# A graph-attention and expert kernel: 14 instead of 15 gathers per source block, and a new order in TensorE's step

## The chip, the cores and the metric

The program runs on one core of a Trainium2 chip. The metric is the time of one execution on the device in microseconds, as the median of several runs. A profile is one execution, taken with the hardware profiler, and has a time of its own.

## The reference

A graph of 6250 nodes with 256 features and 100,000 edges goes through a two-head graph attention layer and then through a layer of eight experts, each with a layer norm ahead and a residual.

```python
x = x + gat(layernorm(x), edge_index)      # W: 256 -> 2 heads of 128
x = x + ffn(layernorm(x))                  # 256 -> 1024, gelu, 8 experts

# gat
Wh = (x @ W_w + W_b).reshape(N, H, D)
s, t = Wh @ a[:D], Wh @ a[D:]
e = leaky_relu(s[src] + t[dst], 0.2)
alpha = softmax of e over the edges of each src
agg = segment_sum(alpha * Wh[dst], src)    # nodes without edges keep Wh

# ffn
H = gelu(x @ W1 + b1)
probs = softmax(H @ Wg + bg)
out = probs[best] * (H @ Wd[best] + bd[best])   # the best expert only
```

The edges come sorted by dst, and dst is skewed to low numbers: about a fifth of the edges go to the first 256 nodes.

## The kernel before

**Preparation.** The edges are spread over the 128 partitions, and each partition sorts its own by source block (128 source nodes) and dst. Meanwhile every node's projected row, with its attention factors, goes to a table in HBM (260 floats a row).

**The edge loop.** The 49 source blocks are worked one after the other. For each, an indirect DMA fetches the 44 keys of every partition that belong to the block (`window`, L615). Up to four edges per partition that go to hot nodes (dst below 256) are handled as counts, without a gather (`pick_pairs`, `count_pairs`, `weigh_pairs`, `add_pairs`). The others are gathered from the table, one indirect DMA for 128 edges, one per partition: a column. There are T = ND + NC columns. The first ND = 12 hold a partition's first 12 edges "in place". What a partition has beyond these is "late": late edges of all partitions are counted (`prefix`), ranked, and packed into NC = 3 more columns of 128 slots. `split` (L657) makes a 0/1 matrix `pick` of late slots by partition, `gather_late` (L733) multiplies it with the keys on TensorE, one product for each late column, and `choose` (L740) takes the one key out of every row and writes its dst and its place.

`spread` (L758) transposes the places on TensorE, stores them in HBM and loads them back broadcast to all partitions (`lbc`). `compare` (L769) makes a 0/1 matrix of it, and `factors` (L773) multiplies this with the source terms; `factor_sums` (L782) adds up their three parts. `fetch` (L788) issues the gathers in three thirds, split at QS, into one of five `wg` buffers of five columns. `compare_back` and `weigh` scale the gathered rows, and `add_up` (L828) sums them by source node, two records on TensorE for each column.

**The expert work.** Four blocks make a group k. When its last block is finished (slot v), the group is normed, transposed (`g_turn`), multiplied with W1 (`g_hidden`), its expert is chosen, and its rows are transposed (`g_rows`) and sent to lists by expert (`g_send`). `tabulate` (L1065) finds which list tiles are full. Such tiles are loaded (`w_load`), transposed (`w_turn`), multiplied with their expert's weights (`w_expert`) and turned into output rows (`w_out`, L1151), which for all but the last two groups go to a waiting place and are sent at the end.

**The order.** No scheduler orders this. Every piece is entered with `at(slot, place, fn, ...)`, the list is sorted by slot and then place, and each engine and each DMA queue works its instructions in that order. A block takes three slots: u = 3 b. Within a slot the places run from about 5 to 81. So for block b: `gather_late` in slot u - 3, `choose` and `spread` in u - 2, `compare`, `factors` and `count_pairs` in u, `factor_sums` in u + 1, and thirds of `fetch` in u, u + 1 and u + 2, of `weigh` one slot and of `add_up` three slots later. At the end `judge` (L719) checks that no block has more late edges than slots (NS = NC x 128); if one has, the program runs a general path after the common one.

Of the kernel before, what the change touches and what calls it, by code (L numbers as in the profile page):

```python
# [10 lines left out]
F32 = mybir.dt.float32  # L11
# [12 lines left out]
P = 128  # L24
# [12 lines left out]
def common_path(  # L37
# [30 lines left out]
    NX = Wg.shape[1]  # L68
# [10 lines left out]
    assert KR * KQ == ES  # L79
    HB, HK = 2, 4  # L80
    HOT = HB * P
    ND, NC, WIN = 12, 3, HK + 40
    NR = WIN - HK - ND
    KS = ES + WIN
    NS = NC * P
# [9 lines left out]
    NPH = -(-(NB - 1) // FB) + 1  # L95
# [6 lines left out]
    NMAX = 2 * NX  # L102
# [91 lines left out]
    with ExitStack() as edges:  # L194
# [3 lines left out]
        def at(slot, place, fn, *args):  # L198
            plan.append((slot, place, len(plan), fn, args))

        kp = edges.enter_context(tc.tile_pool(name="keyp", bufs=2))
# [3 lines left out]
        fw = edges.enter_context(tc.tile_pool(name="ffnw", bufs=2))  # L205
# [118 lines left out]
        bufs = [None] + [keyb if i % 2 == 0 else keya[:, :ES] for i in range(len(steps))]  # L324
# [186 lines left out]
        for i, (d, flip) in enumerate(steps):  # L511
            t = 11 + 1.7 * i if i < 18 else 41.6 + 1.02 * (i - 18)
# [16 lines left out]
        for f0, f1, t0, step in ((n0, n1, 8.0, 0.7), (n4, NB - 1, 15, 2.0)):  # L529
            for j, b in enumerate(range(f0, f1)):  # L530
                c = b % CH
                t = t0 + step * (j - 0.5 * c)
# [11 lines left out]
        for b in range(NB):  # L544
            t = XN0 + NODE * b
# [194 lines left out]
        def choose(b):  # L740
            k = kept[b]
            loc, dsti = k["loc"], k["dsti"]
            pk = k["pm"][:, :NC * (NR + 1)].rearrange("p (c r) -> p c r", c=NC)
            col = kp.tile([P, NC], F32, name="col")
            nc.vector.tensor_sub(col, slot_of, pk[:, :, NR])
            hit = kp.tile([P, NC, NR], F32, name="hit")
            nc.vector.tensor_tensor(hit, iota_s[:, :NR].unsqueeze(1).to_broadcast([P, NC, NR]),
                                    col.unsqueeze(2).to_broadcast([P, NC, NR]), op=ALU.is_equal)
            nc.vector.tensor_mul(hit, hit, pk[:, :, :NR])
            got = kp.tile([P, NC], F32, name="got")  # L750
            nc.vector.tensor_reduce(got, hit, AX.X, ALU.add)
            got_i = got.bitcast(I32)
            nc.vector.tensor_scalar(dsti[:, ND:], got_i, 8, 0x1FFF, op0=ALU.logical_shift_right, op1=ALU.bitwise_and)
            late_i = kp.tile([P, NC], I32, name="late_i")
            nc.vector.tensor_single_scalar(late_i, got_i, 255, op=ALU.bitwise_and)
            nc.scalar.copy(loc[:, ND:], late_i)
# [308 lines left out]
        def tabulate(k, n, last):  # L1065
# [14 lines left out]
            shift = fw.tile([P, NX], F32, name="shift")  # L1080
            nc.vector.tensor_sub(shift, done, upto[:, :NX])
            nc.vector.tensor_add(done, shift, upto[:, 1:])
            past = fw.tile([P, NMAX, NX + 1], F32, name="past")[:, :n]
            nc.vector.tensor_tensor(past, upto.unsqueeze(1).to_broadcast([P, n, NX + 1]),
                                    iota_s[:, :n].unsqueeze(2).to_broadcast([P, n, NX + 1]), op=ALU.is_le)
            tab_f = fw.tile([P, 2, NMAX], F32, name="tab_f")[:, :, :n]
            nc.vector.tensor_reduce(tab_f[:, 0, :], past[:, :, 1:], AX.X, ALU.add)
            which = fw.tile([P, NMAX, NX], F32, name="which")[:, :n]
            nc.vector.tensor_sub(which, past[:, :, :NX], past[:, :, 1:])
            pickd = fw.tile([P, NMAX, NX], F32, name="pickd")[:, :n]  # L1090
            nc.vector.tensor_mul(pickd, which, shift.unsqueeze(1).to_broadcast([P, n, NX]))
            nc.vector.tensor_reduce(tab_f[:, 1, :], pickd, AX.X, ALU.add)
            nc.vector.tensor_add(tab_f[:, 1, :], tab_f[:, 1, :], iota_s[:, :n])
# [96 lines left out]
        for b in range(NB):  # L1190
            u = 3 * b
            at(u - 6, 46, window, b)
            at(u - 4, 24, measure, b)
            at(u - 4, 43, prefix, b)
            at(u - 3, 5, prefix_out, b)
            at(u - 3, 12, split, b)
            at(u - 3, 33.7, gather_late, b)
            at(u - 2, 17, pick_pairs, b)
            at(max(u - 1, -0.2), 63, load_terms, b)
            at(u, 56, scale_terms, b, 0)  # L1200
            at(u + 1, 56, scale_terms, b, 1)
            at(u, 34, count_pairs, b)
            at(u + 2, 51, weigh_pairs, b)
            at(u + 4, 31, add_pairs, b)
            at(u - 2, 16, choose, b)
            at(u - 2, 33.5, spread, b)
            at(u, 9, compare, b)
            at(u, 33, factors, b)
            at(u + 1, 47, factor_sums, b)
            at(u + 4, 62, owned, b)  # L1210
            at(u + 6, 13, owned_biased, b)
            for q in range(3):
                at(u + q, 30, fetch, b, q)
                at(u + q + 1, 48, compare_back, b, q)
                at(u + q + 1, 50, weigh, b, q)
                at(u + q + 3, 32, add_up, b, q)
            at(u + 6, 14, finish, b)

        worked = n_off = 0
        u = [3 * blocks_of(k)[-1] + 6 for k in range(NPH)]  # L1220
        for k in range(NPH):
# [35 lines left out]
            for i in range(n):  # L1257
                t = v + 15 + i if last else u[k + 1] + (5 + 8 * i // n if k < NPH - 2 else (10, 11, 12, 13, 14)[i])
                at(t - 1 if last else t - 2 if k == NPH - 2 else max(t - 3, v + 15), 46 if last else 64, w_load, k, i)
                at(t, 21, w_turn, k, i)  # L1260
                at(t + 1, 22, w_expert, k, i)
                at(t + 2, 30 if k < NPH - 2 else 36, w_out, k, i)
                at(t + 2, 45, w_send if k >= NPH - 2 else w_wait, k, i)
        at(v + 18, 47, judge)
        for j in range(-(-n_off // 2)):
# [539 lines left out]
```

## Time and profile before

| what | us |
|---|---|
| median of three runs | 1344.82 |
| lowest and highest | 1343.49, 1346.52 |
| the profiled execution | 1348.73 |
| its span, first to last instruction | 1346.9 |
| gathers (L792): first and last start | 114.7, 1193.1 |

The span falls into three parts: the preparation up to the first gather, the edge loop with the expert work of earlier groups beside it, and a tail after the last gather, which holds the last group. Between starts of a block's window gather (L619) at 265.9 and 1067.8 lie 36 blocks in 801.9 us, 22.3 us a block. Granted clock of TensorE: 0.924 on the mean, 0.82 between 265.9 and 353.6 us, 0.98 between 708.6 and 796.3 us.

In the profile a gather's row on GpSimd (POOL) is the time in which GpSimd makes the DMA; the transfer itself is not in it. "Issue" as a reason for idle time means that the engine waited for nothing that the profile shows. A matmul in float32 shows as two records on TensorE, each with a weight load (PEld).

### The profile page before, as it was taken

What the parts mean: (1) busy time and instruction counts of PE and PEld (TensorE: products, weight loads), DVE (VectorE), ACT (ScalarE), POOL (GpSimd) and SP (SyncE); (2) the same over time, 40 slices, a digit from 0 to 9 for tenths busy, and PEclk for the clock granted to TensorE, in tenths of its full rate; (3) what the DMA queues carried; (4) which work ended last, traced back from release to release, by engine and by line L of the source; (5) the groups of instructions that cost most, each with busy time, mean ns of one, the idle gap of its engine ahead of it and who ended that gap; (6) DMA issues with size and microseconds to landing.
All of it is one profiled execution on the core that took longest, in us unless ns stands there. A gap on an engine that the chain in (4) does not pass through costs nothing. (4 is left out here: it accounts for less than half of the span.)

```text
span 1346.9 us, 22461 instructions
## 1 busy us (share of the span) xinstructions
PE 1130.7 (84%) x6404; PEld 864.5 (64%) x6404; DVE 945.8 (70%) x3521; ACT 694.2 (52%) x2060; POOL 877.9 (65%) x990
## 2 busy tenths in 40 slices
PE   4683667777986998989979989899898998998997
PEld 3462555556674775775856757757676677585785
DVE  6986877868687787786777876968777779652311
ACT  4683344544645455546465565564645555645321
POOL 0005777777777777776777777777776767736362
PEclk9796887897997998998999999999998899899998
DMA  4764776765656566665766656666657566646871
GB/s 143 220 198 133 228 208 168 207 195 152 187 156 204 182 204 181 221 180 178 219 208 186 216 172 199 198 203 202 213 178 208 158 193 190 182 155 236 296 251 54
DMA packets 118428, 257.91 MB, mean 191 GB/s; under 512 B 24254, under 2 KB 70538, under 8 KB 118152
## 3 DMA queue, kind: packets, MB, share of 16 engines
q0 software_dynamic: 46544, 137.57, 34.2%
q1 hardware_dynamic: 64440, 111.76, 26.3%
q10 hardware_dynamic: 7312, 7.05, 1.6%
q8 instruction: 55, 0.90, 0.3%
q14 instruction: 77, 0.63, 0.2%
HBM read 205.03 MB, written 57.98 MB: 195 GB/s over the span
## 5 line engine op out<-in xcount | busy, mean ns | idle before, releaser
L792 POOL DMA_INDIRECT wg<-table,dsti x735 | 717.0, 976 | 238.4 <-issue 190.4
L833 PE MATMUL p_a<-wg,hot 128*128 128x258 f32 x1470 | 365.5, 399 | 0.0
L833 PEld LDWEIGHTS p_a<-wg,hot 128*128 128x128 f32 x1470 | 286.5, 201 | 52.0 <-issue 9.2
L826 ACT ACTIVATE wg<-wg 128x128 f32<-128x128 f32 x735 | 230.9, 390 | 4.8
L916 PE MATMUL pf<-xT,w_sb 128*128 128x512 f32 (+1 forms) x416 | 200.1, 630 | 22.7 <-ACT xT L908 22.7
L1146 PE MATMUL pf<-wd_sb,half 128*128 x880 | 206.3, 388 | 0.0
L1146 PEld LDWEIGHTS pf<-wd_sb,half 128*128 128x128 f32 x880 | 163.9, 191 | 37.0 <-issue 11.6
L824 ACT COPY wg<-fix 128x10 f32<-128x10 f32 x147 | 25.0, 170 | 297.0 <-DVE wg L823 232.2
L916 PEld LDWEIGHTS pf<-xT,w_sb 128*128 128x128 f32 x416 | 81.3, 210 | 109.5 <-issue 80.6
L809 DVE TENSOR_TENSOR hot<-fix,loc 128x640 f32<-128x640 f32 x147 | 119.1, 810 | 32.7 <-ACT wg L824 32.7
L823 DVE TENSOR_TENSOR wg<-wg,fix 128x640 f32<-128x640 f32 x147 | 120.7, 821 | 5.1
L918 ACT ACTIVATE hT<-pf,b_sb 128x512 f32<-128x512 f32 (+1 forms) x104 | 67.9, 659 | 55.1 <-PE pf L916 54.9
L1040 ACT COPY half<-pf 128x512 f32<-128x512 f32 x110 | 61.4, 585 | 65.9 <-PE pf L1146 34.3
L1040 ACT COPY row<-pf 128x512 f32<-128x512 f32 x94 | 52.4, 586 | 55.0 <-PE pf L1039 54.5
L1060 POOL DMA_INDIRECT by_expert<-row,place_i x47 | 46.8, 996 | 51.1 <-ACT half L1040 17.5
L771 DVE TENSOR_SCALAR lbc<-lbc,iota_p 128x1920 bf16<-128x1920 bf16 x49 | 36.1, 737 | 61.2 <-DMA lbc<-lrow 61.2
L456 PE MATMUL pf<-w_sb,xT 128*128 128x260 f32 x196 | 61.1, 441 | 19.0 <-ACT xT L450 19.0
L704 ACT ACTIVATE wt<-tm,hot_e 128x128 f32<-128x128 f32 x196 | 66.5, 386 | 8.1 <-DMA tm<-terms 8.1
L1039 PE MATMUL pf<-ident,hT 128*128 128x128 f32 x392 | 59.3, 289 | 13.3 <-ACT row L1040 13.2
L619 POOL DMA_INDIRECT win<-keys,first x49 | 48.5, 989 | 32.1 <-DMA keys<-keyb 14.2
L1039 PEld LDWEIGHTS pf<-ident,hT 128*128 128x128 f32 x392 | 46.8, 148 | 21.3 <-ACT row L1040 18.5
L1039 PE MATMUL pf<-ident,row 128*128 128x128 f32 x312 | 45.2, 283 | 18.1 <-DVE y L1160 12.4
(274 smaller groups left out, 1746.9 us busy)
## 6 DMA issues: line engine op xcount, KB each, us to landing
row<-by_expert SPq DMA_DIRECT2D x39, 641.0 KB
lbc<-lrow SPq DMA_DIRECT2D x49, 480.0 KB
wg<-table,dsti POOLq DMA_INDIRECT x735
wg<-by_expert SPq DMA_DIRECT2D x16, 641.0 KB
wd_sb<-in_L_ffn_Wd_dram SPq DMA_DIRECT2D x8, 1024.0 KB
tm<-terms SPq DMA_DIRECT2D x49, 128.0 KB
table<-tb ACTq DMA_DIRECT2D x12, 520.0 KB
xs<-in_x_dram SPq DMA_DIRECT2D x12, 512.0 KB
```

The source lines that it names most:

```text
L456: nc.tensor.matmul(pW[:, :TW], xT[:, k * P:(k + 1) * P], w_sb[:, k, :], start=(k == 0), stop=(k == KC - 1))
L704: nc.scalar.activation(kept[b]["wt"][:, g, h, :], tm[:, h, :], AF.Identity, scale=hot_e[:, g, 1, h:h + 1])
L792: nc.gpsimd.indirect_dma_start(out=wg[:, t - QS[q], :], out_offset=None, in_=table[:, :], in_offset=bass.IndirectOffsetOnAxis(ap=kept[b][" ...
L809: nc.vector.tensor_tensor(hot[:, :n], iota_ps.unsqueeze(1).to_broadcast([P, n, P]), kept[b]["loc"][:, QS[q]:QS[q + 1]].unsqueeze(2).to_bro ...
L823: nc.vector.tensor_mul(wg[:, :, :D], wg[:, :, :D], p_w[:, :, 0:1].to_broadcast([P, n, D]))
L826: nc.scalar.activation(wg[:, t, D2:SE], wg[:, t, D2:SE], AF.Identity, scale=wg[:, t, D + 1:D2])
L833: nc.tensor.matmul(sums[b], hot[:, t - QS[q], :], wg[:, t - QS[q], :SE], start=(t == 0), stop=(t == T - 1))
L916: nc.tensor.matmul(ph[:, :w], wt["w1"][:, k, j * P:(j + 1) * P], xT[:, k, :w], start=(k == 0), stop=(k == KC - 1))
L918: nc.scalar.activation(hT[:, j, :w], ph[:, :w], AF.Gelu, bias=wt["b1"][:, j:j + 1])
L1039: nc.tensor.transpose(pT[:, j * P:(j + 1) * P], rows(4 * h + j), ident)
L1040: nc.scalar.copy(o, pT)
L1146: nc.tensor.matmul(py[:, :C], res[k]["half", i, j // 4][:, j % 4, :], wt["wd"][:, ds(wo[0] + j * C, C)], start=False, stop=(j == KH - 1))
```

## The change

ND goes from 12 to 8 and NC from 3 to 6: T from 15 to 14 columns, NS from 384 to 768 late slots, NR, the keys of a partition that can be late, from 28 to 32. The thirds of `fetch` stay 5, 5 and, now, 4 columns, so columns 8 and 9, the first two late ones, come in the second third. Four work tiles have one buffer instead of two. Six entries of the order move within their slot: `gather_late` from place 33.7 to 40, `spread` from 33.5 to 40, `factors` from 33 to 42, `count_pairs` from 34 to 43, `factor_sums` from 47 to 10, and `w_out`, for all groups but the last two, from 30 to 11.

```diff
-    ND, NC, WIN = 12, 3, HK + 40
+    ND, NC, WIN = 8, 6, HK + 40
     NR = WIN - HK - ND
     KS = ES + WIN
     NS = NC * P
...
-            hit = kp.tile([P, NC, NR], F32, name="hit")
+            hit = kp.tile([P, NC, NR], F32, name="hit", bufs=1)
...
-            past = fw.tile([P, NMAX, NX + 1], F32, name="past")[:, :n]
+            past = fw.tile([P, NMAX, NX + 1], F32, name="past", bufs=1)[:, :n]
...
-            which = fw.tile([P, NMAX, NX], F32, name="which")[:, :n]
+            which = fw.tile([P, NMAX, NX], F32, name="which", bufs=1)[:, :n]
...
-            pickd = fw.tile([P, NMAX, NX], F32, name="pickd")[:, :n]
+            pickd = fw.tile([P, NMAX, NX], F32, name="pickd", bufs=1)[:, :n]
...
-            at(u - 3, 33.7, gather_late, b)
+            at(u - 3, 40, gather_late, b)
...
-            at(u, 34, count_pairs, b)
+            at(u, 43, count_pairs, b)
...
-            at(u - 2, 33.5, spread, b)
+            at(u - 2, 40, spread, b)
             at(u, 9, compare, b)
-            at(u, 33, factors, b)
-            at(u + 1, 47, factor_sums, b)
+            at(u, 42, factors, b)
+            at(u + 1, 10, factor_sums, b)
...
-                at(t + 2, 30 if k < NPH - 2 else 36, w_out, k, i)
+                at(t + 2, 11 if k < NPH - 2 else 36, w_out, k, i)
```

## The prediction

> **What bounds the kernel now.** I read the page's first lines, then the costliest groups, then windows cut where a block begins, then the waits of GpSimd and TensorE inside those windows, and last TensorE's timeline over one block. The page comes first only to see that no engine looks full.
>
> ```profile
> span 1346.9 us, 22461 instructions
> ...
> PE 1130.7 (84%) x6404; PEld 864.5 (64%) x6404; DVE 945.8 (70%) x3521; ACT 694.2 (52%) x2060; POOL 877.9 (65%) x990
> ```
>
> GpSimd at 65% is misleading. Its gathers are the group with the largest busy time, and the idle time ahead of them is nearly all "issue", that is, no other engine is named:
>
> ```profile
> L792 POOL DMA_INDIRECT wg<-table,dsti x735 | 717.0, 976 | 238.4 <-issue 190.4
> L833 PE MATMUL p_a<-wg,hot 128*128 128x258 f32 x1470 | 365.5, 399 | 0.0
> ```
>
> In the timeline one gather starts each 1.25 us: 0.95 us busy and 0.30 us of issue. So a stretch with 70 GpSimd instructions is full at about 87.5 us. I cut windows at every fourth window gather (L619), since the feed-forward work returns every four blocks. The columns are length, then busy time and count of each engine, then clock and DMA:
>
> ```profile
> 353.60:440.80 87.20, 71.65 (x408) 53.17 (x407) 66.86 (x253) 46.58 (x140) 66.90 (x70) 0.88 0.58 175
> 708.60:796.30 87.70, 78.69 (x478) 60.35 (x477) 68.14 (x257) 48.67 (x142) 66.31 (x71) 0.98 0.65 201
> 796.30:886.00 89.70, 80.60 (x488) 61.41 (x487) 69.00 (x258) 50.34 (x150) 65.89 (x70) 0.98 0.63 197
> ```
>
> The first is GpSimd's pace and nothing else; TensorE has 15.6 us to spare. In the other two TensorE is busy 79 to 81 us of 88 to 90. Over the long middle stretch (266 to 1068 us) the waits of GpSimd and of TensorE are:
>
> ```profile
> POOL wg L792 <- issue: 138.1, 448, 0.8
> POOL wg L792 <- ACT wg L824: 9.6, 14, 1.8
> POOL by_expert L1060 <- ACT row L1055: 4.6, 3, 2.4
> ```
>
> ```profile
> PE pm L761 <- ACT loc L756: 23.8, 11, 5.7
> PE pf L916 <- ACT xT L908: 17.6, 9, 2.0
> PE pf L1039 <- DVE y L1160: 11.1, 7, 2.3
> PE pm L779 <- DVE lbc L771: 9.0, 3, 4.5
> ```
>
> GpSimd hardly waits, so it sets the pace. TensorE waits little and is second, close behind. The timeline shows what its steps cost and where it waits for the late places (L761):
>
> ```profile
> 862.96 2.34 PE L833 MATMUL p_a<-wg,hot 128*128 128x258 f32 x10
> 865.13 0.52 PE L779 MATMUL pm<-src_term,lbc 128*128 128x6 bf16 x15
> 865.51 0.83 PE L738 MATMUL pm<-rest,pick 128*128 128x29 f32 x6
> 866.18 0.61 PE L691 MATMUL pm<-places,dests 128*128 128x128 bf16 x8
> ...
> 871.80 0.28 PE L761 MATMUL pm<-ident,loc 128*15 128x128 f32 x1 [1.89 <-ACT loc L756]
> ```
>
> **What the Trainium skill says.** "DMA: Bandwidth & Descriptors", section "SWDGE vs HWDGE vs iDMA", says that GpSimd builds the descriptors of its DMAs in software, and indirect DMAs are its own. The trace agrees: 0.95 us of GpSimd per gather whatever else runs. "TensorE: Matmul & The Clock Gate", section "LDWEIGHTS", says that a weight load costs by its columns. The trace agrees: the six late-rank records (29 moving columns, 128 weight columns) start 0.67 us ahead of the next group, 0.11 us each, as the 128-column transposes of L1039 do in the tail (8 in 0.87 us). So a late column is paid by its weights. "Perfetto Trace Analysis", section "Identifying the Most-Contended Engine", warns that TensorE's busy share is no good measure of its room; I therefore work with its waits.
>
> **The change, part by part.**
>
> GpSimd: 49 gathers less (735 to 686), 1.25 us each: 61 us of its queue, 5.0 us per four blocks.
>
> TensorE, per block: the gather's two records go, at 0.217 us each (ten from 862.96 to 865.13), -0.43 us; one of 15 factor matmuls goes, 0.38 us / 15, -0.03 us. Three late-rank products of two records each are added at 0.11 us, +0.67 us; 33 columns instead of 29 cost nothing while the weights set the pace. Sum +0.21 us a block, +0.84 us per four.
>
> VectorE, per block, by slopes between rows of the by-form groups (384 elements 422 ns and 28 elements 181 ns for a TENSOR_SCALAR; 128 elements 347 ns and 384 elements 621 ns for a SCALAR_TENSOR_TENSOR; 84 elements 248 ns and 640 elements 810 ns for a TENSOR_TENSOR): the two picks over 768 columns +0.26 and +0.41 us; three operations over 192 elements instead of 84, +0.11 us each; the last third's two wide operations over 512 instead of 640 elements, -0.13 us each; compare -0.05 us. Sum +0.7 us. ScalarE loses one 0.39 us scaling. VectorE is busy 68 us of 88, so I charge nothing; the cover is its own waits (48 us for lbc and 43 us for the late counts in the middle stretch). Without the cover it would be 2.8 us per four blocks.
>
> One buffer instead of two (hit, past, which, pickd): all their readers and writers are VectorE, in order. Nothing.
>
> spread from 33.5 to 40: it issues a transpose, a ScalarE copy and two DMAs on SP. Between the two places nothing is issued on SP or GpSimd (GpSimd's fetch is at 30, its send at 44, SP's store at 45), so it passes only g_fold, g_count, g_turn and g_rows on TensorE and their copies on ScalarE. In the slot after a group is finished, VectorE runs the norm and the table ahead of choose, and TensorE stood 1.8 us for loc with transposes ready behind it; these now go first. The price is a later lbc: spread to compare takes about 8 us where compare waits (899.3 to 907.4), and spread moves some 2.5 us later in two of four blocks. Compare would then wait 1 to 2 us more there, ahead of split; the late-count wait that follows takes most of it.
>
> gather_late, factors and count_pairs to 40 to 43: none of them issues a DMA, and in their slot nothing of TensorE lies between the old and new places except in the last group. Late ranks now precede factors, so choose's input comes no later than 0.3 us. Nothing.
>
> factor_sums from 47 to 10: it waits for factors, the end of TensorE's slot before. Queued behind are w_out, choose and pick_pairs, and spread waits for choose. But choose waited for the same end already. I take 0; bounds 0 and +0.6 us a block (the count_pairs group, if it waits for that too).
>
> w_out from 30 to 11: its PSUM buffer comes free before choose or split runs, not after. TensorE's waits for "DVE y" are 2.1 us of the period at 708 to 796 us (1.6 at L1039, 0.5 at L903). I let both go; bounds 0 and -2.1 us.
>
> The late columns are now in the second third's gathers (columns 8 and 9), a slot sooner. The late places (L756) were ready 10 us or more before that fetch in every block but the first, where it was 5. Nothing.
>
> **The sum.** Between 705 and 800 us the groups of TensorE show 9.1 us of waits: 2.0 for xT, 1.4 for row copies, 2.5 at the row transposes, 1.8 for loc, 0.5 and 0.7 at L903 and L1144, 0.2 at L650. The change takes 1.8 + 2.1 = 3.9 us, so TensorE needs 87.7 - 3.9 + 0.84 = 84.6 us. GpSimd would need 87.5 - 5.0 = 82.5 us. TensorE ends last there: -3.1 us per dense period. Blocks 2 to 8 (seven) and 9 to 16 (eight) have TensorE to spare: 15 x 1.25 = 18.8 us. Blocks 0 and 1, part of it: 1 us. Blocks 17 to 48 are eight dense periods: 8 x 3.1 = 24.8 us. Head (to 115 us) and tail (from 1194 us, a chain of expert products) are as before. Sum 44.6 us. The profiled execution took 1348.7 us (span 1346.9 and 1.8 around it), 3.9 above the median of the runs. 1348.7 - 44.6 = 1304.1; against the median 1344.8 - 44.6 = 1300.
>
> **Rivals.** (A) The forecast, TensorE takes over: 1300, own range 1288 to 1312. Chance 0.50.
>
> (B) GpSimd stays the bound since TensorE's busy time is partly drain: 61.5 us plus about half of the 14 us in which GpSimd now waits for others, 1276; with all of it 1269. For it: L779's 0.52 us group leaves room for the next after 0.38. Against: four waits of TensorE stay. 0.20.
>
> (C) The moves free nothing and TensorE keeps its 9 us of waits: -19.8 + 8 x 0.84 = -13, so 1332. For it: xT and the row copies are not touched, and VectorE now stands at the head of each slot. 0.18.
>
> (D) Slower: the late places sit last in TensorE's slot, lbc lands later, compare is first in VectorE's slot and holds split, and the products last in TensorE's slot then wait for split and compare. This decides once TensorE's waits per dense period grow from 9.1 by over 1.6 us (19.8 / 8 - 0.84). At 1 us a block, +4: 8 x 4.84 - 19.8 = +19, so 1364. For it: compare waited 17 times, up to 4.5 us. Against: after it VectorE waits for the late counts anyway. 0.10.
>
> (E) A block's late edges overflow its 768 slots and the general path runs: from the inputs the fullest block has 760. 0.02, far slower.
>
> **Numbers.** About 0.2% (2.7 us) is what can be told from no change. A, B and nearly all of C are faster: 0.86; same 0.03; slower 0.11. The range, 1270 to 1328, holds A, B and half of C.
>
> **What would show it.** 686 gathers still 1.25 us apart early; a window of four blocks near 82.5 us at 350 us and 84 to 85 us after 600 us; the loc wait of TensorE under 5 us in the middle stretch, the DVE y wait gone, xT as before; GpSimd waiting for ScalarE and TensorE more than now. If the dense windows read 82.5, B; if 88 with TensorE's waits kept, C; if lbc and L738 waits grow, D.

## The result and the profile after

| | before | after |
|---|---|---|
| median of 22 runs | 1346.25 us | 1352.35 us |
| lowest and highest | 1337.12, 1354.38 | 1338.90, 1358.21 |
| ratio after to before, 95% interval | | 1.0041 (1.0019 to 1.0063) |
| the profiled execution, its span | 1348.73, 1346.9 | 1348.91, 1347.1 |

The changed kernel is slower by 0.4%, where 1300 us was forecast. The two profiled executions lie nearer together than the medians do (0.2 us against 6.1), so the traces below show where the expected 44.6 us went, not all of the 6 us.

The page of the changed kernel, first lines and the two groups that were shown of before:

```profile
span 1347.1 us, 22591 instructions
...
PE 1141.0 (85%) x6551; PEld 878.2 (65%) x6551; DVE 974.3 (72%) x3521; ACT 675.3 (50%) x2011; POOL 840.9 (62%) x941
...
L792 POOL DMA_INDIRECT wg<-table,dsti x686 | 675.0, 984 | 260.8 <-issue 192.4
L833 PE MATMUL p_a<-wg,hot 128*128 128x258 f32 x1372 | 345.5, 401 | 0.0
```

The work moved as written: GpSimd (POOL) 37 us less, TensorE (PE) 10 us and VectorE (DVE) 28.5 us more. Windows of four blocks, cut at the window gathers as before (length first, then each engine's busy time and count):

```profile
341.70:425.20 83.50, 69.74 (x385) 53.06 (x385) 67.65 (x244) 44.33 (x134) 64.13 (x67) 0.90 0.58 175
696.80:787.90 91.10, 82.14 (x501) 63.05 (x500) 70.05 (x256) 49.26 (x147) 62.58 (x67) 0.98 0.60 183
787.90:880.20 92.30, 83.03 (x496) 63.85 (x496) 70.93 (x258) 48.32 (x144) 62.98 (x66) 0.94 0.60 184
```

The first is GpSimd's new pace, 67 instructions of 1.25 us, down from 87.2. The dense windows were 87.7 and 89.7 and became 91.1 and 92.3. A block is taken to start at its window gather. Block by block: block 17 starts 15.6 us earlier than before (425.2 against 440.8), block 45 only 7.6 us earlier (1060.2 against 1067.8), block 48 4.1 us, the last scatter 5.4 us (1332.5 against 1337.9), and the end of the span 0.2 us later. So there are two losses: 11.5 us in the dense part, and 5.6 us behind the last scatter.

Waits of TensorE in the middle stretch (258.3 to 1060.2 us, as long as the stretch of before, 801.9 us): total, times, longest:

```profile
PE pf L916 <- ACT wg L824: 17.5, 9, 2.0
PE pm L738 <- DVE place_i L666: 13.8, 4, 4.0
PE pf L1039 <- DVE y L1160: 13.0, 7, 3.5
PE pf L903 <- ACT row L1040: 12.0, 9, 1.6
```

The wait for the late places (L761, 23.8 us before) and the one for lbc (L779, 9.0 us) are gone. In their place stand the late-rank products waiting for `split` (L738) and the transposes of `g_turn` waiting for a row copy (L903); the y wait of L1039 grew from 11.1 to 13.0. But the four waits at L738 all lie between 293 and 398 us, ahead of block 17. In blocks 17 to 44, where the forecast looked for its gain, the picture is simpler. The kernel before first (440.8 to 1067.8 us), then the changed kernel (425.2 to 1060.2 us), each with its window:

```profile
440.80:1067.80 627.00, 566.07 (x3359) 432.17 (x3358) 478.31 (x1797) 345.19 (x1012) 466.46 (x491) 0.96 0.65 197
...
PE pm L761 <- ACT loc L756: 11.5, 6, 2.1
PE pf L1039 <- DVE y L1160: 11.1, 7, 2.3
```

```profile
425.20:1060.20 635.00, 571.54 (x3438) 438.81 (x3437) 492.67 (x1792) 333.65 (x985) 443.41 (x463) 0.95 0.61 187
...
PE pf L1039 <- DVE y L1160: 13.0, 7, 3.5
PE pf L903 <- ACT row L1040: 10.7, 7, 1.6
```

The late-place wait of 11.5 us went, and a row-copy wait of 10.7 us came. All gaps of TensorE together were 60.9 us before and are 63.5 after (the window less its busy time). TensorE stood at half clock for 51.2 us of this stretch before and for 58.0 after; that can explain 3.4 us of the 8.0 at most.

The y wait in one of its seven cases. The y of `w_out` (L1160) stands right behind `compare` (L771), and `compare` waits for lbc; in all seven it waited about 1.0 us or more there:

```profile
644.58 0.69 DVE L771 TENSOR_SCALAR lbc<-lbc,iota_p 128x1792 bf16<-128x1792 bf16 x1 [3.31 <-DMA lbc<-lrow]
...
645.24 0.47 DVE L1160 SCALAR_TENSOR_TENSOR y<-pf,row 128x256 f32<-128x256 f32 x1
645.77 1.11 PE L1039 MATMUL pf<-ident,row 128*128 128x128 f32 x4 [3.52 <-DVE y L1160]
```

GpSimd in the middle stretch (258.3 to 1060.2 us) waits more for ScalarE (9.6 us before), as it should if it no longer sets the pace:

```profile
POOL wg L792 <- issue: 141.3, 415, 4.6
POOL wg L792 <- ACT wg L824: 22.5, 9, 6.6
```

VectorE's waits in blocks 17 to 44, again the kernel before first:

```profile
DVE lbc L771 <- DMA lbc<-lrow: 41.7, 14, 4.5
DVE pick L662 <- ACT late L653: 33.2, 13, 4.0
DVE hot L809 <- ACT wg L824: 19.5, 15, 3.6
DVE col L745 <- PE pm L738: 9.6, 7, 1.9
```

```profile
DVE lbc L771 <- DMA lbc<-lrow: 54.7, 26, 5.5
DVE hot L809 <- ACT wg L824: 23.9, 14, 3.6
DVE fs L786 <- PE pm L691: 19.6, 7, 3.2
DVE pick L662 <- ACT late L653: 9.2, 8, 2.8
```

The forecast counted the waits for lbc and for the late counts as room for VectorE's new work. The second did shrink, by 24.0 us. But lbc comes later and costs 13.0 more, and `factor_sums`, now at place 10, waits 19.6 for the end of TensorE's step. In the kernel before `choose` (L745) waited for that end, but only 9.6 us, also seven times: 10.0 of the 19.6 are new. The record that `factor_sums` waits for is of `count_pairs` (L691), which now stands last in the step. All in all VectorE was busy 14.4 us longer there (492.7 against 478.3) and idle 6.4 us less; the stretch grew by 8.0.

One slot shows how a wait moves. It is the slot after a group's end. TensorE in the kernel before:

```profile
777.52 1.11 PE L717 MATMUL p_a<-hot_x,wt 128*128 128x129 f32 x8
...
782.63 0.28 PE L761 MATMUL pm<-ident,loc 128*15 128x128 f32 x1 [1.82 <-ACT loc L756]
...
789.06 5.40 PE L916 MATMUL pf<-xT,w_sb 128*128 128x512 f32 x8 [1.95 <-ACT xT L908]
```

TensorE and then ScalarE in the changed kernel:

```profile
769.61 1.11 PE L717 MATMUL p_a<-hot_x,wt 128*128 128x129 f32 x8
...
774.48 0.63 PE L903 MATMUL pf<-ident,xnf 128*128 128x128 f32 x4 [0.71 <-DVE col L745]
776.61 0.66 PE L903 MATMUL pf<-ident,xnf 128*128 128x128 f32 x4 [1.50 <-ACT row L1040]
777.11 0.65 PE L1039 MATMUL pf<-ident,hT 128*128 128x128 f32 x4
778.43 0.66 PE L1039 MATMUL pf<-ident,hT 128*128 128x128 f32 x4 [0.68 <-ACT row L1040]
...
781.17 5.40 PE L916 MATMUL pf<-xT,w_sb 128*128 128x512 f32 x8 [1.98 <-ACT wg L824]
```

```profile
775.88 0.20 ACT L756 CAST loc<-late_i 128x6 f32<-128x6 int32 x1 [0.80 <-DVE late_i L755]
775.98 1.07 ACT L1040 COPY row<-pf 128x512 f32<-128x512 f32 x2
```

TensorE no longer stands for the late places, since their transpose went behind `g_turn` and `g_rows`. But these need PSUM buffers, the buffers come free by ScalarE's row copies, and ahead of the copies in ScalarE's queue stands the cast of the same late places, waiting for VectorE. From the start of `add_pairs` (L717) to that of the first W1 products (L916) the slot lasted 11.54 us before and lasts 11.56 now. (The wait at L916 is the one for xT in both: the copies of xT end at 781.12, and L824, which the line names, at the same moment.)

The end of the span, GpSimd's last instructions (minimum, median and longest in ns), before and after:

```profile
L1800 POOLq DRAIN  x3: 40/107/3332, 1342.8 to 1346.7; - x3
```

```profile
L1800 POOLq DRAIN  x3: 40/107/7987, 1338.3 to 1346.9; - x3
```

The last drain took 3.33 us and takes 7.99, and the instruction ahead of it 2.13 us instead of 0.99: 5.8 us more. Both are the same, to 0.01 us, in every kernel below with 686 gathers, and as before in every one with 735.

### The profile page after: what moved, and what is told of

It reads as the page before. It is cut to its first block, busy times and chain, and to the rows that moved or that the text cites. A ratio compares the mean times of both kernels' runs of the same rounds, so it can differ in the third digit from the quotient of the medians.

```text
span 1347.1 us, 22591 instructions
## 1 busy us (share of the span) xinstructions
PE 1141.0 (85%) x6551; PEld 878.2 (65%) x6551; DVE 974.3 (72%) x3521; ACT 675.3 (50%) x2011; POOL 840.9 (62%) x941
## 3 DMA queue, kind: packets, MB, share of 16 engines
q1 hardware_dynamic: 64342, 110.14, 25.8%
## 4 chain that ended last, share of the span: by engine, by line
PE 52%; DVE 17%; DMA 13%; ACT 9%; issue 4%; POOL 3%; ACTq 0%; PEld 0%; SPq 0%; DVEq 0%; POOLq 0%; PEldq 0%
PE p_a L833 13%; PE pf L916 11%; PE pf L1146 10%; DMA lbc<-lrow 6%; PE pf L1039 4%; PE pm L738 4%; DMA wg<-table,dsti 3%; PE p_a L717 2%; DMA lrow<-lT 2%; POOL wg L792 2%; DVE wg L823 2%; PE pf L456 1%; ACT wg L826 1%; ACT row L1040 1%; PE pm L691 1%
## 5 line engine op out<-in xcount | busy, mean ns | idle before, releaser
L792 POOL DMA_INDIRECT wg<-table,dsti x686 | 675.0, 984 | 260.8 <-issue 192.4
L833 PE MATMUL p_a<-wg,hot 128*128 128x258 f32 x1372 | 345.5, 401 | 0.0
L833 PEld LDWEIGHTS p_a<-wg,hot 128*128 128x128 f32 x1372 | 269.1, 202 | 49.5 <-issue 8.6
L826 ACT ACTIVATE wg<-wg 128x128 f32<-128x128 f32 x686 | 216.6, 390 | 4.8
L916 PE MATMUL pf<-xT,w_sb 128*128 128x512 f32 (+1 forms) x416 | 199.1, 627 | 23.2 <-ACT wg L824 19.3
L824 ACT COPY wg<-fix 128x10 f32<-128x10 f32 x147 | 24.4, 166 | 270.6 <-DVE wg L823 205.6
L916 PEld LDWEIGHTS pf<-xT,w_sb 128*128 128x128 f32 x416 | 81.1, 210 | 110.9 <-issue 79.7
L809 DVE TENSOR_TENSOR hot<-fix,loc 128x640 f32<-128x640 f32 x147 | 112.3, 764 | 31.5 <-ACT wg L824 31.5
L823 DVE TENSOR_TENSOR wg<-wg,fix 128x640 f32<-128x640 f32 x147 | 114.1, 776 | 5.1
L738 PEld LDWEIGHTS pm<-rest,pick 128*128 128x128 f32 x588 | 80.3, 209 | 35.1 <-issue 32.8
L738 PE MATMUL pm<-rest,pick 128*128 128x33 f32 x588 | 78.4, 288 | 28.2 <-DVE place_i L666 28.2
L1040 ACT COPY half<-pf 128x512 f32<-128x512 f32 x110 | 60.9, 584 | 76.4 <-PE pf L1039 42.4
L1060 POOL DMA_INDIRECT by_expert<-row,place_i x47 | 50.2, 1069 | 62.0 <-issue 21.3
L771 DVE TENSOR_SCALAR lbc<-lbc,iota_p 128x1792 bf16<-128x1792 bf16 x49 | 34.4, 703 | 72.7 <-DMA lbc<-lrow 72.7
L456 PE MATMUL pf<-w_sb,xT 128*128 128x260 f32 x196 | 61.5, 443 | 18.8 <-ACT xT L450 18.7
L1039 PE MATMUL pf<-ident,hT 128*128 128x128 f32 x392 | 58.9, 287 | 19.4 <-ACT row L1040 13.2
```

Source lines behind the costliest of these rows:

```text
L456: nc.tensor.matmul(pW[:, :TW], xT[:, k * P:(k + 1) * P], w_sb[:, k, :], start=(k == 0), stop=(k == KC - 1))
L738: nc.tensor.matmul(pk[:, c, :], k["pick"][:, c * P:(c + 1) * P], k["rest"], start=True, stop=True)
L792: nc.gpsimd.indirect_dma_start(out=wg[:, t - QS[q], :], out_offset=None, in_=table[:, :], in_offset=bass.IndirectOffsetOnAxis(ap=kept[b][" ...
L809: nc.vector.tensor_tensor(hot[:, :n], iota_ps.unsqueeze(1).to_broadcast([P, n, P]), kept[b]["loc"][:, QS[q]:QS[q + 1]].unsqueeze(2).to_bro ...
L823: nc.vector.tensor_mul(wg[:, :, :D], wg[:, :, :D], p_w[:, :, 0:1].to_broadcast([P, n, D]))
L826: nc.scalar.activation(wg[:, t, D2:SE], wg[:, t, D2:SE], AF.Identity, scale=wg[:, t, D + 1:D2])
```

## The experiments

All runs below fell on five chips on which the kernel before takes 1661 to 1683 us, not 1346. Each is compared with the kernel before on its own chip, run beside it; none of the parts was run where the kernel before takes 1346 us. No chip is on record at both speeds. So "the first chip" stands below for the conditions of the first comparison, and that the chip itself makes the difference is not shown. There the change looks different: on the three of them where it ran, the changed kernel is faster.

The page and the clock of the changed kernel on one of these chips:

```profile
span 1647.2 us, 22591 instructions
...
PE 1264.3 (77%) x6551; PEld 950.2 (58%) x6551; DVE 978.7 (59%) x3521; ACT 681.2 (41%) x2011; POOL 833.3 (51%) x941
```

```profile
core 0: 1647.2 us, clock 0.849
```

TensorE's timeline there, inside one group of expert products:

```profile
798.05 2.21 PE L1146 MATMUL pf<-wd_sb,half 128*128 x9
800.56 0.46 PE L1146 MATMUL pf<-wd_sb,half 128*128 x1 [0.30 <-issue]
801.97 0.46 PE L1146 MATMUL pf<-wd_sb,half 128*128 x1 [0.95 <-issue]
804.08 0.38 PE L1146 MATMUL pf<-wd_sb,half 128*128 x1 [1.65 <-issue]
805.54 2.35 PE L1146 MATMUL pf<-wd_sb,half 128*128 x4 [1.08 <-issue]
```

On the first chip no group of products is broken like this. A pause is counted here when TensorE idles over 0.15 us between two records of one line and the same tiles and the trace names nothing that it waited for. In the run shown (e0_after) the pauses come to 122.5 us, 146 of them; in the first comparison's profiles of both kernels there are none. (The traces of these chips hold fewer semaphore records, 11148 against 25422 for the same program, so some pauses can be waits whose end was not recorded; 47.9 us of them lie inside groups of L717 and L779, whose inputs are complete when the group starts.) The granted clock stands at half for 497 us of the span, against 197 us for the same kernel on the first chip. The Trainium skill, "TensorE: Matmul & The Clock Gate", section "Part 1: The HAM clock gate (the "warmup" mystery)", says that the array runs at half rate after it was idle and at full rate after a few us of work. The clock records agree that there are only these two values. Here the half rate began at 805.0, in the last of four pauses that together took 3.98 of 5.28 us; there was no single long idle stretch. What makes the pauses is open.

The pauses are in the last column below, summed over the one profiled execution of each run. One kernel's sum differs between chips by 31 to 44 us (the changed kernel 122.5, 103.3 and 134.1; new columns with the old order 140.4, 96.7 and 127.2). Effects of 10 to 40 us are no larger than that, so where two runs differ in their pauses too, the pauses are a rival to every other reading of the difference. The kernel before was not profiled on these chips. In g1_gp, g2_pe, g3_both, i2_first and i3_busy some edges are missing from the result.

| run | kernel | median, before beside it | ratio, 95% interval | pauses, us |
|---|---|---|---|---|
| e0_after | the changed kernel | 1634.85, 1682.52 | 0.9731 (0.9685 to 0.9778) | 122.5 |
| f0_after | the changed kernel | 1613.91, 1661.01 | 0.9729 (0.9681 to 0.9776) | 103.3 |
| j0_after | the changed kernel | 1634.97, 1678.76 | 0.9728 (0.9687 to 0.9769) | 134.1 |
| e1_cols | new columns, old order | 1656.23, 1682.52 | 0.9858 (0.9816 to 0.9899) | 140.4 |
| f1_cols | the same | 1621.74, 1661.01 | 0.9779 (0.9732 to 0.9825) | 96.7 |
| g4_cols | the same | 1648.21, 1677.11 | 0.9814 (0.9759 to 0.9869) | 127.2 |
| e2_order | old columns, new order | 1675.83, 1682.52 | 0.9963 (0.9920 to 1.0006) | 121.6 |
| e3_twice | before, late-rank products twice | 1721.07, 1682.52 | 1.0236 (1.0186 to 1.0285) | 174.8 |
| h1_again | the second pass one slot later | 1727.13, 1680.56 | 1.0285 (1.0241 to 1.0329) | 98.7 |
| g1_gp | before, 15th gather replaced | 1616.00, 1677.11 | 0.9643 (0.9593 to 0.9693) | 109.6 |
| i3_busy | the same, GpSimd kept as long | 1615.72, 1678.76 | 0.9645 (0.9599 to 0.9691) | 117.7 |
| g2_pe | before, 15th product left out | 1674.21, 1677.11 | 0.9997 (0.9973 to 1.0021) | 143.0 |
| i2_first | before, 5th product left out | 1678.49, 1678.76 | 0.9966 (0.9931 to 1.0001) | 133.9 |
| g3_both | g1_gp and g2_pe together | 1622.18, 1677.11 | 0.9678 (0.9623 to 0.9732) | 111.7 |
| f2_cast | changed kernel, cast moved | 1633.31, 1661.01 | 0.9843 (0.9803 to 0.9882) | 104.1 |
| f3_bf16 | changed kernel, late ranks in bf16 | 1639.73, 1661.01 | 0.9887 (0.9844 to 0.9930) | 151.4 |
| h2_shift | changed kernel, late-rank stage a slot later | 1620.10, 1680.56 | 0.9653 (0.9617 to 0.9689) | 61.8 |
| j1_shift | the same | 1623.39, 1678.76 | 0.9663 (0.9617 to 0.9709) | 65.2 |

Four theories stood. Theory 1: after block 17 TensorE sets the pace, by its own work and by waits that no place in the order removes. Theory 2, the forecast's rival D: the late `spread` makes lbc late and holds VectorE. Theory 3: GpSimd alone sets the pace. Theory 4, formed on the way: each of a block's three slots has its own bound.

### The change in its two parts

The new columns with the six places of before, the new places with the columns of before, and, as a diff, late-rank products made twice in the kernel before (e3_twice):

```diff
             for c in range(NC):
-                nc.tensor.matmul(pk[:, c, :], k["pick"][:, c * P:(c + 1) * P], k["rest"], start=True, stop=True)
+                for _ in range(2):
+                    nc.tensor.matmul(pk[:, c, :], k["pick"][:, c * P:(c + 1) * P], k["rest"], start=True, stop=True)
```

> The changed kernel again, beside the others on one chip. All theories: 1.002 to 1.006 of before, so +3 to +9 us. It is the base for the other runs.

> The new columns (8 in place, 6 late) with the old order. Theory 1 (TensorE sets the pace after block 17 with its own occupancy plus waits that no place in the order removes): GpSimd gains 15 to 19 us before block 17, TensorE pays 0.21 us a block and choose comes 0.3 to 1 us later for each group of four: between -6 and +3 us against before. Theory 2 (the late place of spread makes lbc late and holds VectorE): with spread early again this is clearly faster than before, -10 to -20 us.

> The old columns (12 in place, 3 late) with the new order. Theory 1: GpSimd's 15 gathers set the pace and TensorE's waits only change places: -4 to +4 us. Theory 2: the order itself costs, +6 to +15 us. The forecast's own step (the order frees 3.9 us of TensorE in each group of four): TensorE gets room, GpSimd stays at 87.5 us a group, -5 to -10 us.

> The kernel before with each late-rank product made twice: TensorE gets six more records a block (+0.67 us), GpSimd and VectorE nothing. Theory 1: in blocks 17 to 48 TensorE is at par with GpSimd, so most of 32 x 0.67 = 21 us shows, +12 to +22 us. Theory 3 (GpSimd alone sets the pace of the kernel before, TensorE's busy time is partly drain): 0 to +5 us.

> The changed kernel once more, as the base for the three runs beside it, and to see whether its standing against the kernel before depends on the chip. Where the kernel before takes about 1346 us and TensorE's matmuls show no pauses inside a group, 2 to 9 us slower than before, as in the first comparison. Where the kernel before takes about 1680 us and TensorE pauses inside its groups, 40 to 55 us faster, as in the second.

> New columns (eight in place, six late), all six steps at their old places in the order. Theory 1, TensorE sets the pace after block 17 by its own work and by waits that no place in the order removes: within 6 us of the changed kernel where before takes about 1346 us. Theory 2, the late spread makes lbc late and holds VectorE: 10 to 20 us below the changed kernel. The forecast's own step, the order takes waits away: 10 to 31 us above the changed kernel. Where before takes about 1680 us: 15 to 28 us above the changed kernel, as before.

> New columns at the old places once more, for the case that this chip is like the first. Where before takes about 1346 us: Theory 1: 0 to 8 us slower than before (TensorE's waits stay, its work grows by 0.21 us a block, GpSimd's gain ends at block 17); the forecast's own step (the order takes the waits away): 19.8 us gained before block 17 and 8 x 0.84 lost after it, 10 to 16 us faster than before; Theory 2 (late spread costs): 10 to 20 us faster than before. Where before takes about 1660 us: 0.978 to 0.986 of it, as before.

The first set of expectations was written for a chip like the first, and the change itself missed it: 47.7 us faster, and 47.1 and 43.8 on two more chips. The columns are worth 26, 39 and 29 us of it. The order, with the new columns, is worth 21.4 us on one chip and 7.8 on another (15 to 28 were expected), and the intervals of the second overlap; with the old columns 6.7 us, inside the 5 to 10 that the forecast's own step gave, but in an interval that holds no change. So the order gains something on one chip and perhaps on the others. Theory 2 is not borne out there: the old places, `spread`'s earlier one among them, made no kernel faster. But the six places were moved together, so a small cost of the late `spread` could lie hidden under the gain of the others. 0.67 us of late-rank products more in each block (33 us in all) cost 38.5 us, more than any theory gave (12 to 22 us, or 0 to 5); this run also has the largest sum of pauses.

### One engine relieved at a time

On the kernel before, first GpSimd alone (g1_gp), then TensorE alone (g2_pe), and both (g3_both). The runs without a product also have the closing test for empty sums set so that the general path is not started (not shown):

```diff
-            for t in range(QS[q], QS[q + 1]):
+            for t in range(QS[q], min(QS[q + 1], T - 1)):
                 nc.gpsimd.indirect_dma_start(
...
+        def fetch_plain(b):
+            nc.sync.dma_start(out=rows[b, 2][0][:, HT - 1, :], in_=table[b * P:(b + 1) * P, :])
...
+                if q == 2:
+                    at(u + q, 46.5, fetch_plain, b)
```

```diff
-            for t in range(QS[q], QS[q + 1]):
+            for t in range(QS[q], min(QS[q + 1], T - 1)):
                 nc.tensor.matmul(sums[b], hot[:, t - QS[q], :], wg[:, t - QS[q], :SE],
-                                 start=(t == 0), stop=(t == T - 1))
+                                 start=(t == 0), stop=(t == T - 2))
```

> The kernel before with GpSimd relieved alone: the fifteenth gather of a block is no longer GpSimd's; a plain load of 128 consecutive table rows on SyncE's queue fills its place, as many bytes, so the edges of that column are left out of the result and other rows stand in. TensorE, VectorE and ScalarE do all that they did. Theory 3 (GpSimd alone sets the pace): 45 to 61 us below before (49 x 1.25). The forecast: about 35 to 45 below. Theory 1 (TensorE sets the pace after block 17): only blocks 2 to 16 gain, 12 to 22 us below before where before takes about 1346 us; where it takes about 1660 us and TensorE pauses, within 8 us of before.

> The kernel before with TensorE relieved alone: the product of a block's fifteenth column (one matmul of two records, 0.43 us) is left out, and so are its edges' sums; the gather and all else stay. Theory 1: 33 blocks x 0.43 = 14, so 8 to 16 us below before where before takes about 1346 us; where it takes about 1660 us and TensorE pauses, 15 to 35 us below (49 x 0.43 = 21 and the pauses that go with it). Theory 3 (GpSimd alone): 0 to 3 us below.

> Both at once: no fifteenth gather on GpSimd (a plain load stands in) and no product of it on TensorE. It is what the change removes, without what it adds. Theory 1: the sum of the two, 25 to 38 us below before where before takes about 1346 us, and what the product alone brings, within 8 us, where before takes about 1660 us. Theory 3: 45 to 61 us below.

49 gathers less gain 61.1 us, 1.25 us each, and both reliefs together gain no more (54.9). 0.43 us of TensorE less in each block gains nothing that can be told (15 to 35 us were Theory 1's). Theory 1 falls as a statement about TensorE's total work: taking work away gains nothing, though adding it costs.

Is it GpSimd's queue, then? `i3_busy` keeps the plain load and gives GpSimd two memsets in the gather's stead; `i2_first` relieves TensorE in the slot where the late-rank products stand. The first diff is on top of g1_gp, the second on the kernel before.

```diff
+        def busy():
+            for _ in range(2):
+                nc.gpsimd.memset(filled, 0.0)
...
+                    at(u + q, 30.5, busy)
```

```diff
+                if t != 4:
-                nc.tensor.matmul(sums[b], hot[:, t - QS[q], :], wg[:, t - QS[q], :SE],
+                    nc.tensor.matmul(sums[b], hot[:, t - QS[q], :], wg[:, t - QS[q], :SE],
...
```

> As the run that relieved GpSimd alone (the fifteenth gather replaced by a plain load on SyncE's queue, its edges left out; 61 us below before), but GpSimd stays as long: two memsets of a scratch tile (128x641, about 0.6 us each) stand where the gather stood. Theory 3 for the gather's share (it was GpSimd's queue that counted): the gain goes, within 10 us of before. If it was the indirect transfer itself, its descriptors and scattered reads, and not the queue: 45 to 61 us below before, as without the memsets.

> The kernel before with the product of a block's fifth column left out (0.43 us of TensorE, in the third of the block in which the late-rank products stand; its edges' sums are left out), the gather and all else kept. The product of the fifteenth column, in another third, brought nothing. Theory 4 (each third has its own bound): 15 to 30 us below before where before takes about 1660 us, 5 to 15 where it takes about 1346. GpSimd holds every third: within 5 us of before.

> The changed kernel as the base for the run beside it: 0.973 of before where before takes about 1660 us, 1.002 to 1.006 of it on a chip like the first.

The groups of GpSimd in i3_busy (busy in total, mean ns of one):

```profile
L792 POOL DMA_INDIRECT wg<-table,dsti x686 | 666.1, 971 | 385.0 <-issue 204.1 <-PE pf L1047 59.6 <-ACT rest L655 29.9
L802 POOL MEMSET filled<- 128x641 bf16 x98 | 63.5, 648 | 2.8
```

GpSimd spent 66 us on the memsets, more than the 61 of the gathers, and the gain stayed whole: 63.0 us. So on these chips the queue of GpSimd is not what counts. GpSimd waits behind that place anyway, over 1 us in 40 of the 49 blocks. In one of them:

```profile
710.09 1.35 POOL L802 MEMSET filled<- 128x641 bf16 x2
717.06 1.00 POOL L1068 DMA_INDIRECT by_expert<-row,place_i  x1 [5.62 <-ACT row L1063]
```

What the gain belongs to is the indirect transfer itself, or that the third's last column no longer comes by one; which of its consumers was held up stays open. Theory 3 fails with its reason, though its number came out. And TensorE's relief gains nothing in this slot either (0.3 us).

### Where the late-rank products stand

On the kernel before, the second pass in the next slot (h1_again); on the changed kernel, the whole late-rank stage a slot later (h2_shift, j1_shift):

```diff
+        def gather_again(b):
...
+                nc.tensor.matmul(pk[:, c, :], k["pick"][:, c * P:(c + 1) * P], k["rest"], start=True, stop=True)
...
             at(u - 2, 33.5, spread, b)
+            at(u - 2, 34.5, gather_again, b)
```

```diff
-            at(u - 3, 40, gather_late, b)
+            at(u - 2, 34, gather_late, b)
...
-            at(u - 2, 16, choose, b)
-            at(u - 2, 40, spread, b)
-            at(u, 9, compare, b)
+            at(u - 1, 16, choose, b)
+            at(u - 1, 40, spread, b)
+            at(u, 31, compare, b)
```

> The kernel before with the late-rank products of a block made twice, as in the earlier run (38.6 us slower), but the second pass stands in the next slot of the three (place 34.5, behind the transpose of the late places) and nobody reads it. TensorE does exactly as much more work. Theory 4 (each third of a block has its own bound: the late-rank products stand in the third in which VectorE waits for TensorE's end, and what is spent there can't be given back in the other two): 0 to 12 us slower than before. Theory 1 (TensorE's total work sets the pace): 30 to 45 us slower where before takes about 1660 us, 12 to 22 where it takes about 1346.

> The changed kernel with the late-rank stage one slot later: the products at place 34 of the slot after (in place of 40 of the slot before), choose, spread and compare one slot later too. The same instructions, on the same engines. Theory 4: the 1.33 us of late-rank products leave the slot for whose end VectorE waits, 20 to 60 us below the changed kernel where before takes about 1660 us, 5 to 30 where it takes about 1346. Theory 1: within 8 us of the changed kernel (0.973 of before, or 1.004 of it on a chip like the first). If the later spread makes compare wait for lbc, it is slower than the changed kernel instead.

> The changed kernel with the late-rank stage one slot later, beside the changed kernel itself: 5 to 20 us below it (0.965 of before against 0.973 in different calls). If within 5 us, the shift brings nothing that can be told.

The second pass costs 46.6 us in the other slot, no less than the 38.5 in the first: Theory 4 falls with it and with `i2_first`. The late-rank stage a slot later (`compare` moves only within its slot, from place 9 to 31) is 0.7 to 0.8% under the changed kernel: 11.6 us on the chip where both ran, with intervals that overlap slightly, and about the same ratio on another. It is the fastest version that was run with a whole result. No theory gave the size (20 to 60 us, or within 8). Its pauses, 65.2 us against 134.1 of the changed kernel on the same chip, fell by more than the gain; what the shift itself is worth was not separated from them.

### The two remedies that failed

Both on the changed kernel, first the cast (f2_cast), then the products in bf16 (f3_bf16):

```diff
-            nc.scalar.copy(loc[:, ND:], late_i)
+            k["late_i"] = late_i
...
+            at(u - 2, 39.5, cast_late, b)
```

```diff
+            high = rest.bitcast(BF16)[:, 1::2]
+            nc.vector.tensor_sub(low, rest, high)
+            nc.vector.tensor_copy(mid, low)
+            nc.vector.tensor_sub(end, low, mid)
...
-                nc.tensor.matmul(pk[:, c, :], k["pick"][:, c * P:(c + 1) * P], k["rest"], start=True, stop=True)
+                for i, part in enumerate(k["parts"]):
+                    nc.tensor.matmul(pk[:, c, :], k["pick"][:, c * P:(c + 1) * P], part, start=(i == 0), stop=(i == 2))
```

> The changed kernel with one ScalarE instruction moved: the cast of the late places (L756) stands no longer in choose (place 16) but at place 39.5, behind the row copies of the same slot. Theory 1 with its reason (that cast waits for VectorE in ScalarE's queue, ahead of the copies that give TensorE its PSUM buffers back): the waits of TensorE at L903 for the row copy go, 10 us in blocks 17 to 44, and the time is 3 to 10 us below the changed kernel. Theory 2 (late lbc): within 3 us of it.

> The changed kernel with the late-rank products in bf16: the row of packed values is cut into three bf16 parts on VectorE (three small operations more, about 0.5 us a block), and each late column takes three bf16 products that add up in PSUM, in place of one float32 product of two records. By the spacing of the bf16 records of L779 (0.035 us) against 0.11 us, 18 records take 0.6 to 0.7 us in place of 1.3 to 1.4. Theory 1 (TensorE's own work sets the pace after block 17): 15 to 34 us below the changed kernel. Theory 2 (VectorE is held and sets the pace): 0 to 10 us above it, by VectorE's 0.5 us a block. Theory 3 (GpSimd alone sets the pace): within 4 us of it.

Moving the cast behind the row copies made it 19.4 us slower than the changed kernel. Its one profiled execution was also its fastest (1618.99 us), so the trace can't show where. In it the row-copy waits at the transposes of `g_turn` are shorter, as was meant, but not gone (13.7 us against 19.0 of the changed kernel), and the pauses are the same (104.1 and 103.3 us). That the cast delays the row copies is to be read in the traces; that taking it out of the way would help is not shown.

The busy lines of the changed kernel on that chip and of f3_bf16:

```profile
PE 1245.3 (77%) x6551; PEld 936.3 (58%) x6551; DVE 977.8 (60%) x3521; ACT 678.3 (42%) x2011; POOL 836.0 (52%) x941
```

```profile
PE 1208.9 (74%) x6845; PEld 887.6 (54%) x6845; DVE 1008.2 (62%) x3668; ACT 678.3 (41%) x2011; POOL 843.1 (52%) x941
```

The late-rank products took 25 us of TensorE instead of 74, from the start of each record to the next, idle time not counted. VectorE took 30 us more, in `split`, ahead of the picks. The kernel became 25.8 us slower, where Theory 2 gave 0 to 10 and Theory 1 a gain. ScalarE is unchanged and GpSimd makes the same gathers. Two costs are left. One is VectorE's part, 0.62 us a block, which the forecast would have charged nothing; 25.8 us would be 0.53 a block. (Its first operation also needs ScalarE's late rank ahead of the picks, where only the products needed it before.) The other is TensorE's pauses: with 294 records more they grew from 103.3 to 151.4 us, by about as much as the products saved. The costs were not separated, so this run does not show that VectorE's part was paid.

## Why the prediction was wrong

**What was right.** GpSimd set the pace up to block 17: 83.5 us per four blocks (82.5 forecast), and 15.6 of the 18.8 + 1 us came. TensorE's own work grew much as forecast: in blocks 17 to 44 its busy time rose by 5.5 us, against 28 x 0.21 = 5.9. The agreement is in part luck: the late-rank products added 16.7 us there, not 18.8, and the transposes of the late places 2.2, which the forecast had not counted (gather products -11.7). Over all 49 blocks six late-rank records took 0.76 us a block on the mean and twelve take 1.43, the 0.67 more of the forecast. That a record's time is that of its 128 weight columns holds here for float32 (0.10 to 0.11 us apart, with 29 or 33 moving columns); bf16 records with as many weight columns started 0.026 us apart in f3_bf16, so the columns alone don't set it. The wait for xT stayed (17.6 and 17.5), the loc wait went from the dense part, and GpSimd waits more for ScalarE.

**The step that failed: "The change takes 1.8 + 2.1 = 3.9 us"** of TensorE's waits per four blocks, from which came 84.6 us per dense period and 24.8 us in all. The dense part lost 11.5 us instead. The 1.8 us at the late places went, and came back as waits for PSUM buffers at L903 (11.5 us in blocks 17 to 44 before, 10.7 after); the 2.1 us of y waits did not go, since `w_out` at place 11 stands behind `compare` at 9, and `compare` waits for lbc. TensorE's waits in blocks 17 to 44 were to fall by 7 x 3.9 = 27.3 us and rose by 2.5. These 29.8 us are all of what the forecast missed there (7 x 3.1 = 21.7 us of gain against a loss of 8.0). The error was to subtract a wait by its name, without asking what the same instruction waits for next.

**A second step: "so I charge nothing"** for VectorE's +0.7 us a block. Its cover was to be the waits for lbc and the late counts. One shrank by 24 us; the other grew by 13, and the wait for the end of TensorE's step by 10.0 (19.6 for `factor_sums` against 9.6 for `choose`). The latter is 0.36 us a block, inside the forecast's bounds of 0 and 0.6 and for the reason given there: `factor_sums` waits for `count_pairs` too. Of the 14.4 us of new work in blocks 17 to 44 idle time covered 6.4. That VectorE's work makes TensorE's waits longer fits the y waits and the cast, but no run shows it by itself, f3_bf16 included. How much of the first chip's loss is this and how much the order was not separated there.

**A third: the tail "as before".** GpSimd's closing instructions take 5.8 us more with 686 gathers, which ate the 5.4 us that were left at the last scatter.

The sum, against the profiled execution: 36.3 us missed in the dense part (24.8 + 11.5), 4.2 before it (18.8 + 1 - 15.6), 5.6 at the end, and 1.3 gained between block 48 and the last scatter: 44.8, the whole of the forecast gain and 0.2 more.

Of the rivals, C (the moves free nothing, 1332) describes TensorE's waits, and one of D's signs is there in the dense part: VectorE waits 0.46 us a block longer for lbc. The other, late-rank products that wait for `split`, is there only ahead of block 17. D's price of 1 us a block (1364) was not reached on the profile.

On three other chips the change gains 2.7%, close to the forecast's 3.3%. As far as the runs show that is luck: there it is not GpSimd's queue that gives the gain. 61 us go with the fifteenth indirect transfer, 39 to 47 us come back with late-rank products, and the order adds 7 to 21. The parts do not add up (14 to 22 us would remain for the columns, which measured 26 to 39), and TensorE's pauses change along with them. That these parts have the same signs on the first chip is not shown.

## What to carry to other kernels

Where several engines wait for one another in turn, a wait that is moved is not a wait that is saved: follow the waiting instruction to its next input and to the queue that must deliver it before subtracting anything. Don't charge added time on an engine with idle time at nothing until the idle time is shown to be in the same slot and not itself a wait that the added time delays. And a result of half a per cent belongs to the conditions it was measured in: the same kernel was 0.4% slower on one chip and 2.7% faster on three. Before an experiment elsewhere is used to explain it, look whether the same thing limits the kernel there.

## What the runs showed of the hardware

- The same program takes 1346 us in the first comparison and 1661 to 1683 us on five chips. There TensorE pauses inside its groups (103 to 134 us in the changed kernel, none in the first comparison) and its clock stands at half for 497 us (e0_after) instead of 197.
- GpSimd's closing work goes with the kernel's indirect DMAs and not with its time: 0.99 + 3.33 us in every kernel with 735 gathers, 2.13 + 7.99 us in every one with 686, whether the span is 1347 or over 1600 us. Only these two counts were run.
- Eighteen bf16 records of 33 columns with 128-column weights started 0.026 us apart, twelve in float32 0.10 us apart (1.26 us from the first to the next group, as the median of the changed kernel). The kernel with the quicker form was slower.
- GpSimd held by two memsets of 0.65 us in place of a gather of 0.98 us and its 0.30 us of issue left the time as if it were free (0.9645 and 0.9643 of the kernel before).
